# A graph layer paced by its gathers: eight stretches of nine chunks, each with one extra kind of instruction

## The chip, the cores and the metric

One core of one Trainium2 chip runs the kernel. The metric is the device time of one execution in microseconds; the time of a version is the median of its runs. All times below are of this one core.

## The reference

One graph layer with a residual and a normalisation. Each of 1,650,000 edges takes the row of its source node (160 numbers, 64 scalars and 32 vectors of 3), combines it with the edge's four attributes and small weight matrices, and adds the result to its destination node. The edges come sorted by destination: 800,000 in one direction, the same reversed, and 50,000 self-loops.

```
s, v = x[:, :64], x[:, 64:].reshape(n, 32, 3)
ss, vv = s[src], v[src]
e0, e1 = sh[:, 0:1], sh[:, 1:4]
out0 = C0 * (ss * e0 @ W1 + einsum('eui,ei->eu', vv, e1) * INV3 @ W2)
p3 = (ss @ W3)[:, :, None] * e1[:, None, :] * INV3
p4 = einsum('eui,uw->ewi', vv * e0[:, :, None], W4) * INV3
p5 = einsum('eui,uw->ewi', cross(vv, e1[:, None, :]), W5) * INV6
m = concatenate([out0, C1 * (p3 + p4 + p5)])
m_agg = segment_sum(m, dst, n)
h = m_agg through Ws and Wv
x = layernorm(x + x + relu(h))
...
```

## The kernel before

**Units, groups, pairs, chunks.** 128 edges are a unit, 6 units a group (`G`), 2 groups a pair (`PG`), 20 groups a chunk (`SG`), so a chunk has 10 pairs and 120 units. There are 1044 pairs in 105 chunks. The main loop runs over the pairs.

**One pair.** POOL issues 12 indirect DMAs (`gather`, line 398), one a unit: each brings the 128 source rows of a unit, 640 bytes each, into the tile `xg`. The pool of `xg` has four buffers, so POOL can be ahead of PE by that many pairs; each gather adds 16 to a semaphore of its own, `filled[t][j]`, with t the buffer and j the unit. PE multiplies the 12 units one after the other (`group_sums`, line 447) by the matrices `ha`, 128 edges x 128 (4 attributes x 32 slots for the destinations of a group), and sums six of them into one half of `ps`. Each of these matmuls waits for the semaphore of its unit. A matmul in fp32 appears in the profile as two weight loads and two matmuls.

**DVE.** It makes `hot` and `ha` for the next pair (`spread`, lines 419 and 422) while PE works on this one, and turns the sums of the pair before (`turn_sums`, the transpose in line 462) and adds them to `ring`, the running sums of the nodes (line 471). Once a node block of 128 is complete, PE multiplies it by the weights (`phb`, line 776), and DVE and ACT normalise it (`norm1` to `norm3`, lines 184 to 200; the square root `rstd` in line 194 is ACT's) for a store of two blocks at once (`out<-o`, line 875).

**Beside this** goes a second stream of work. Since half of the edges are the other half reversed, the kernel sorts a pack of edges into rows by DVE work (`pack`, copies and predicated copies in lines 590 to 635, with a few casts on ACT) and stores them to memory in many small DMAs on SP (`store`, line 683: `edges<-prow` of 27.8 KB and `selves<-mine` of 0.8 KB). Before a few of these stores SP loads their places into registers (line 666). This phase of stores comes back about every 1600 us.

**Order.** SP, PE, DVE and ACT run in the order in which the code is written (a manual schedule). The body of the loop issues the gathers of a pair, then goes through `group_sums`, a generator that yields after each of the 12 matmuls. After the second, DVE's `turn_sums` of the pair before is written; after the fourth, `spread` for the next pair; after each, some steps of the queued work on node blocks, loads and packs. SP issues all loads and stores of the loop. Its DMAs share eight completion lanes in turn with the few that ACT issues: a DMA waits for the one eight earlier in the program. The loads of a chunk are written 13 pairs before its first pair.

Of the kernel before, what the change touches and what calls it, by code (L numbers as in the profile page):

```python
# [39 lines left out]
F32 = mybir.dt.float32  # L40
# [6 lines left out]
ET = mybir.EngineType  # L47
# [3 lines left out]
P = 128  # L51
MUL0, MUL1 = 64, 32
D = MUL0 + 3 * MUL1
# [10 lines left out]
W = 32  # L64
# [14 lines left out]
REST = 15  # L79
ASK, OWN, QS, RUN = 8, 16, 8, 2  # L80
LEAD = 3

def plan(n_nodes, n_edges):

    nblk = 125
    assert n_nodes % nblk == 0
    assert W == FB
    nb = n_nodes // nblk
    again = 9

    per_unit = P * n_nodes / n_edges
    group = max(g for g in range(1, 17)
                if g == 1 or (g + 0.2) * per_unit + 1 + 5 * math.sqrt(g * per_unit * per_unit / P) <= W)
    head = math.ceil(min(HEAD, n_edges / (group * P)) / SG) * SG
    eh = head * group * P
    row = group * P * 3 // 2 + math.floor(per_unit * group * 3 / 2 * (1 - n_nodes / n_edges))
    assert row * n_nodes / n_edges + 5 * math.sqrt(row * n_nodes / n_edges / 16) < KM

    far = math.ceil(6 * math.sqrt(n_edges) / 2 * n_nodes / n_edges) + 2
    rows = math.ceil((n_edges - eh) / row) + 2  # L100
    ngroups = math.ceil((n_edges - n_nodes + eh * n_nodes / n_edges + far) / (group * P))
    assert eh + (rows - 1) * row - n_nodes + eh * n_nodes / n_edges - far >= ngroups * group * P
    units = P * math.ceil(max(math.ceil(n_edges / P) + again - 1, math.ceil((eh + rows * row + 1) / P)) / P)
    return nblk, nb, again, group, units, ngroups, row, head, rows, far
# [3 lines left out]
def tile_gnn_resnorm(ctx: ExitStack, tc: tile.TileContext, x, src, dst, attr, W1, W2, W3, W4, W5, Ws, Wv, out, n_edges):  # L108
    nc = tc.nc
    N = x.shape[0]  # L110
    NBLK, NB, GA, G, NU, NG, L, NH, NR, FAR = plan(N, n_edges)
# [8 lines left out]
    eps_t = const.tile([P, 1], F32, name="eps_t")  # L120
# [86 lines left out]
    def near(g):  # L207
        p = g * G * P
        return p / degree if p <= EH else EH / degree + (p - EH) / (degree - 1)
# [6 lines left out]
    for g0, g1 in parts:  # L216
        t = min((near(g) / N for g in range(g0, g1 + 1)), key=lambda t: abs(t - 0.5))
# [10 lines left out]
    TW = max(h - k * S for h, k in zip(high, seg_of)) + W  # L228
# [3 lines left out]
    with tc.tile_pool(name="once", bufs=1) as once, tc.tile_pool(name="raw", bufs=2) as rawp, \  # L232
# [5 lines left out]
            tc.tile_pool(name="psP", bufs=1, space=PSUM) as psP, tc.tile_pool(name="psA", bufs=2, space=PSUM) as psA, \  # L238
            tc.tile_pool(name="psM", bufs=2, space=PSUM) as psM, ExitStack() as later_pools:

        spotp, ownp = (later_pools.enter_context(tc.tile_pool(name=name, bufs=bufs))
                       for name, bufs in (("spot", 3), ("own", 1)))
        extremes = once.tile([P, 2, NSC], F32, name="extremes")
        count_ = once.tile([1, SG], F32, name="count")
        nc.gpsimd.iota(count_, pattern=[[1, SG]], base=0, channel_multiplier=0, allow_small_or_imprecise_dtypes=True)
# [7 lines left out]
        dq = nc.sync  # L253
# [56 lines left out]
        spot_of, spots_of, ring = {}, {}, {}  # L310
# [76 lines left out]
        filled = [[tc.alloc_semaphore(f"filled{t}_{j}") for j in range(PG * G)] for t in range(4)]  # L387
        gathers = [[0] * (PG * G) for t in range(4)]
        begun_tiles = [0]

        def gather(s, placed, u, n):

            xg = rowp.tile([P, PG * G, D], F32, name="xg")
            rows = []
            t = begun_tiles[0] % 4
            begun_tiles[0] += 1
            for j in range(n):
                part = nc.gpsimd.indirect_dma_start(  # L398
                    out=xg[:, j, :], out_offset=None, in_=x,
                    in_offset=bass.IndirectOffsetOnAxis(ap=placed[0][:, u + j:u + j + 1], axis=0))  # L400
                gathers[t][j] += 1
                key = f"gather{begun_tiles[0]}_{j}"
                part.then_inc(filled[t][j], 16)
                tc.no_tile_sem_insts.add(part.ins.name)
                tc.add_to_no_dep_group(key, part.ins)
                rows.append((xg[:, j, :], filled[t][j], 16 * gathers[t][j], key))
            return rows

        idle, sent = [], []
# [20 lines left out]
        written = {"misc": [], "ps": []}  # L430

        def fresh(kind):
            written[kind].append([])

        def wrote(kind, ins):
            ws = written[kind]
            for old in ws[-3] if len(ws) > 2 else []:
                tc.declare_no_dep(ins.ins, old, reason="its reader has waited for it")
            ws[-1].append(ins.ins)
            return ins  # L440

        def group_sums(p, rows, ha):

            ps = psA.tile([P, PG, D], F32, name="ps")
            fresh("ps")
            for j, (xr, sem, count, key) in enumerate(rows):
                mm = nc.tensor.matmul(ps[:, j // G, :], ha[:, j].rearrange("p k w -> p (k w)"), xr,  # L447
                                      start=j % G == 0, stop=j % G == G - 1)
                mm.wait_op(sem, count, "sem-ge")
                tc.declare_no_dep(mm.ins, group=key, reason="its own semaphore is waited for")  # L450
                tc.declare_fence(mm.ins, group=key)
                if j % G == 0:
                    wrote("ps", mm)
                else:
                    written["ps"][-1].append(mm.ins)
                yield ps

        def turn_sums(p, ps):
# [15 lines left out]
        C = 2 + NK  # L474
# [4 lines left out]
        def row_start(r):  # L479

            lo, hi = (math.floor(r * L * (1 - 1 / degree)) - 2 * FAR - 2, math.ceil(r * L * (1 - 1 / degree)) + 2 * FAR + 2)
            return (max(lo, 0), hi if r else 0), (max(math.floor((EH + r * L) / degree) - FAR - 2, 0),
                                                  math.ceil((EH + r * L) / degree) + FAR + 2)
# [234 lines left out]
        def own_blocks(k):  # L718

            if min((k + 1) * S, N) <= row_start(0)[1][0]:  # L720
                return []
            return list(range(k * SB, min((k + 1) * SB, nblocks)))
# [48 lines left out]
        def block(bs, h, ph):  # L771
# [3 lines left out]
            for i in range(ND):  # L775
# [4 lines left out]
        pairs = [(s, g, min(PG, NG - g, (s + 1) * SG - g)) for s in range(NSC)  # L780
                 for g in range(s * SG, min(NG, (s + 1) * SG), PG)]

        ones = once.tile([P, P], F32, name="ones")
        nc.vector.memset(ones, 1.0)

# [132 lines left out]
        def reach(s):  # L918

            end = min(NG, (s + 1) * SG) * G * P  # L920
            if s * SG < NH:
                return 0
            if s + 1 < NSC:
                end = max(end, (s * SG * G + P) * P)
            if s * SG == NH:
                end = max(end, (s * SG + W) * G * P)
            return end - EH

        packs, due = [], []
        for i in range(npacks):  # L930
# [3 lines left out]
            own = next((k for k in range(NSEG) if min((k + 1) * S, N) > row_start(i * RP)[1][0] and own_blocks(k)), NSEG - 1)  # L934
            due.append(min((first - 1) * per - 1 - LEAD, first_of[own] // PG - ASK - 1))
            packs.append(pack(i, lambda i=i: reads[i + 1]() if i + 1 < npacks else None))
# [5 lines left out]
        for k in range(1, NSEG):  # L942
            p = first_of[k] // PG
# [5 lines left out]
        for b, g in enumerate(last_of):  # L949
            p = g // PG  # L950
# [6 lines left out]
        for p, (s, g, ng) in enumerate(pairs):  # L957
            if (p + LEAD) % per == 0 and (p + LEAD) // per + 1 < NSC or not p:
                ahead_ = (p + LEAD) // per + 1
                end = reach(ahead_)  # L960
                assert end <= 0 or rows_stored[0] == NR or end <= row_start(rows_stored[0])[0][0]
                raws[ahead_] = load(ahead_)
            if p % per == 0 and s + 1 < NSC:
                after_pair(p + 1, do_cast, s + 1)
                after_pair(p + 2, do_place, s + 1)
                if s + 2 == NSC:
                    after_pair(p + 4, examine_all)
                    after_pair(p + 6, read_flags)
            rows = gather(s, placed[s], (g - s * SG) * G, ng * G)
            for j, ps in enumerate(group_sums(p, rows, has.pop(p))):  # L970
                if j == 1 and turning:
                    turn_sums(*turning)
                    turning = None
                if j == 3 and p + 1 < len(pairs):
                    s1, g1, ng1 = pairs[p + 1]
                    has[p + 1] = spread(placed[s1], (g1 - s1 * SG) * G, ng1 * G)
                work(1.0)
                if packs and p >= START:
                    when = p + (j + 1) / (ng * G)
                    todo = math.ceil(len(packs[0]) * min(1, (when - began) / max(1, due[0] - began)))  # L980
                    for step in packs[0][done:todo]:
                        if step:
                            step()
                    done = max(done, todo)
                    if done == len(packs[0]):
                        packs.pop(0), due.pop(0)
                        done, began = 0, when
# [35 lines left out]
    with tc.tile_pool(name="up", bufs=1) as up, tc.tile_pool(name="us", bufs=2) as us, tc.For_i(0, once_more, 1):  # L1023
# [3 lines left out]
        mm = up.tile([P, 2, JU], F32, name="mm")  # L1027
# [45 lines left out]
    with tc.tile_pool(name="edges2", bufs=2) as ep, tc.tile_pool(name="ops2", bufs=2) as op, \  # L1073
            tc.tile_pool(name="node2", bufs=1) as np_, tc.tile_pool(name="psA2", bufs=2, space=PSUM) as psA, \
            tc.tile_pool(name="psF2", bufs=1, space=PSUM) as psF:
        with tc.For_i(0, blocks, 1) as b:
# [5 lines left out]
            with tc.For_i(u0, u1, GA) as u:  # L1082
# [21 lines left out]
                ps = psA.tile([NBLK, 2, 512], F32, name="ps2")  # L1104
                for j in range(GA):
                    for h in range(2):
                        nc.tensor.matmul(ps[:, h, 0:2 * D], hot[:, j, :], xa[:, j, 2 * h:2 * h + 2, :],
                                         start=j == 0, stop=j == GA - 1)
# [11 lines left out]
            i = 0  # L1120
# [44 lines left out]
```

## Time and profile before

| what | value |
|---|---|
| median of 3 runs | 17920.9 us (17918.87 to 17925.29) |
| the profiled execution | 18022.02 us, span 18020.3 us |
| PE | 6860.2 us, 38% of the span |
| PE's weight loads | 6095.4 us, 34% |
| DVE | 7478.3 us, 41% |
| ACT | 171.6 us, 1% |
| POOL | 11866.1 us, 66% |
| clock of PE granted | 0.627 |
| DMA | 74 GB/s over the span |

The page gives the busy time of each engine; PE's weight loads run beside its matmuls. A group of instructions is listed by line, engine, operation and tiles, with its count, its busy time, the mean of one in ns, and the idle time of the engine just before it with what ended it. "issue" there means that nothing which the profile shows was waited for. `q0` is the queue of the gathers, `q1` that of SP's and ACT's transfers.

By the places of the chunks' first gathers, the stretches that the change touches lie, in us from the start of the span, at 1443 to 2989 (A), 3504 to 5050 (B), 5564 to 7111 (C), 7623 to 9172 (D), 9687 to 11233 (E), 11751 to 13293 (F), 13812 to 15358 (G) and 15874 to 17414 (H).

### The profile page before, as it was taken

What the parts mean: (1) busy time and instruction counts of PE and PEld (TensorE: products, weight loads), DVE (VectorE), ACT (ScalarE), POOL (GpSimd) and SP (SyncE); (2) the same over time, 40 slices, a digit from 0 to 9 for tenths busy, and PEclk for the clock granted to TensorE, in tenths of its full rate; (3) what the DMA queues carried; (4) which work ended last, traced back from release to release, by engine and by line L of the source; (5) the groups of instructions that cost most, each with busy time, mean ns of one, the idle gap of its engine ahead of it and who ended that gap; (6) DMA issues with size and microseconds to landing.
All of it is one profiled execution on the core that took longest, in us unless ns stands there. A gap on an engine that the chain in (4) does not pass through costs nothing. (4 is left out here: it accounts for less than half of the span.)

```text
span 18020.3 us, 93561 instructions
## 1 busy us (share of the span) xinstructions
PE 6860.2 (38%) x28971; PEld 6095.4 (34%) x28972; DVE 7478.3 (41%) x12038; ACT 171.6 (1%) x273; POOL 11866.1 (66%) x12535
## 2 busy tenths in 40 slices
PE   3333334333333333333333333333333333333433
PEld 2233333333333333333333333333333333333333
DVE  7344245334524442453344345434433452444232
ACT  0000000000000000000000000000000000000000
POOL 6566666666666666666666666666666666666666
PEclk6666666666666666666666666666666666666666
DMA  2222322322332233223223322332232233222222
GB/s 72 79 71 78 79 68 73 83 76 70 77 81 70 71 80 77 70 73 85 73 70 78 80 70 72 82 77 69 72 85 74 69 76 78 72 70 71 75 72 61
DMA packets 740962, 1341.57 MB, mean 74 GB/s; under 512 B 243310, under 2 KB 522674, under 8 KB 725894
## 3 DMA queue, kind: packets, MB, share of 16 engines
q0 software_dynamic: 601056, 1026.60, 23.5%
q1 hardware_dynamic: 138138, 308.06, 5.6%
q8 instruction: 231, 3.78, 0.1%
q14 instruction: 273, 2.24, 0.0%
q10 hardware_dynamic: 1264, 0.88, 0.0%
HBM read 1263.28 MB, written 71.42 MB: 74 GB/s over the span
## 5 line engine op out<-in xcount | busy, mean ns | idle before, releaser
L398 POOL DMA_INDIRECT xg<-in_x,si x12522 | 11862.6, 947 | 6108.8 <-issue 3663.5
L447 PE MATMUL ps<-xg,ha 128*128 128x160 f32 x25044 | 6282.8, 397 | 9643.7 <-issue 5600.4
L447 PEld LDWEIGHTS ps<-xg,ha 128*128 128x128 f32 x25044 | 5409.4, 267 | 10356.9 <-issue 10352.3
L462 DVE STREAM_TRANSPOSE sums<-ps 128x320 f32<-128x320 f32 x1044 | 527.0, 505 | 6249.8 <-remote 4712.4
L422 DVE TENSOR_TENSOR ha<-hot,pk 128x1536 f32<-128x1536 f32 x1044 | 1830.4, 1753 | 52.1 <-remote 11.0
L776 PE MATMUL phb<-BWk,ring 128*128 128x160 f32 (+1 forms) x3910 | 1176.4, 381 | 1441.0 <-issue 858.6
L184 DVE SCALAR_TENSOR_TENSOR y<-phb,xt 128x320 f32<-128x320 f32 x196 | 95.9, 489 | 3623.2 <-PE ps L447 2504.7
L776 PEld LDWEIGHTS phb<-BWk,ring 128*128 128x128 f32 (+1 forms) x3910 | 894.1, 258 | 1489.1 <-issue 886.9
L471 DVE TENSOR_TENSOR ring<-ring,sums 128x160 f32 x2087 | 684.5, 328 | 253.1 <-issue 158.6
L419 DVE TENSOR_TENSOR hot<-bank,rel 128x384 f32<-128x384 f32 x1044 | 570.6, 547 | 67.4 <-DMA xt<-in_x 67.3
L632 DVE COPY_PREDICATED prow<-marks,prow 128x2370 f32<-128x2370 int32 (+5 forms) x198 | 550.3, 2780 | 1.1
L766 DVE STREAM_TRANSPOSE ring<-xr 128x1280 f32<-128x1280 f32 x188 | 437.2, 2326 | 0.1
L632 DVE COPY_PREDICATED pra<-marks,pra 128x1580 f32<-128x1580 int32 (+5 forms) x198 | 378.8, 1913 | 0.0
L763 DVE TENSOR_TENSOR xr<-xr,bank 128x1280 f32<-128x1280 f32 x188 | 276.5, 1471 | 4.6 <-DVE bank L756 1.4
L194 ACT ACTIVATE rstd<-mv,eps_t 128x2 f32<-128x2 f32 x196 | 58.0, 296 | 16997.5 <-DVE mv L189 12612.7
L468 DVE TENSOR_TENSOR ring<-ring 128x196 f32<-128x196 f32 (+20 forms) x485 | 149.4, 374 | 1.8
L200 DVE TENSOR_SCALAR o<-y,mv,rstd 128x160 f32<-128x160 f32 x391 | 130.2, 374 | 10.9 <-remote 1.6
L629 DVE COPY_PREDICATED_SCALAR hit<-marks,none 128x395 int32 (+5 forms) x198 | 130.1, 657 | 10.9 <-DVE pri L627 3.2
L716 DVE MEMSET ring<- 128x1280 f32 (+1 forms) x98 | 119.3, 1218 | 23.1 <-issue 21.0
L188 DVE BATCH_NORM_STATS2 st<-y 128x6 f32<-128x160 f32 x391 | 121.7, 311 | 6.7
L630 DVE COPY_PREDICATED hit<-marks,pri 128x395 int32<-128x395 int32 (+5 forms) x198 | 118.5, 598 | 10.4 <-issue 2.2
L627 DVE TENSOR_TENSOR pri<-hit,marks 128x395 int32<-128x395 int32 (+11 forms) x198 | 113.5, 573 | 14.8 <-issue 3.2
(346 smaller groups left out, 1752.7 us busy)
## 6 DMA issues: line engine op xcount, KB each, us to landing
xg<-in_x,si POOLq DMA_INDIRECT x12522
xr<-in_x SPq DMA_DIRECT2D x93, 1280.0 KB
r<-edges SPq DMA_DIRECT2D x100, 384.0 KB
edges<-prow SPq DMA_DIRECT2D x1330, 27.8 KB
xt<-in_x SPq DMA_DIRECT2D x195, 160.0 KB
out<-o SPq DMA_DIRECT2D x195, 160.0 KB
pra<-in_attr SPq DMA_DIRECT2D x10, 2370.0 KB
selves<-mine SPq DMA_DIRECT2D x1328, 0.8 KB
```

The source lines that it names most:

```text
L200: nc.vector.tensor_scalar(o[:n, i], y[:n, i], mv[:n, i, 0:1], rstd[:n, i:i + 1], op0=ALU.subtract, op1=ALU.mult)
L398: part = nc.gpsimd.indirect_dma_start(out=xg[:, j, :], out_offset=None, in_=x, in_offset=bass.IndirectOffsetOnAxis(ap=placed[0][:, u + j:u ...
L419: idle[:] = [nc.vector.tensor_tensor(hot[:, :n], slotsP[:, 0:W].unsqueeze(1).to_broadcast([P, n, W]), rel[:, u:u + n].unsqueeze(2).to_broa ...
L422: nc.vector.tensor_tensor(ha[:, :n], hot[:, :n].unsqueeze(2).to_broadcast([P, n, NK, W]), pk[:, :, u:u + n].rearrange("p k u -> p u k").un ...
L447: mm = nc.tensor.matmul(ps[:, j // G, :], ha[:, j].rearrange("p k w -> p (k w)"), xr, start=j % G == 0, stop=j % G == G - 1)
L462: nc.vector.transpose(at[:, :ng], ps[:, :ng].rearrange("p g (b f) -> p g b f", f=FB))
L468: nc.vector.tensor_tensor(ring[k][:, b, :past], ring[k][:, b, :past], ring[k - 1][:, b, S:S + past], op=ALU.add)
L471: nc.vector.tensor_tensor(here, here, at[:, i], op=ALU.add)
L632: nc.vector.copy_predicated(what[:n, a:e], mi[:, r].unsqueeze(2).to_broadcast([n, e - a, what.shape[2]]), what[:n, a + d:e + d])
L763: nc.vector.tensor_tensor(xr[:, r], xr[:, r], sumP[:, r].unsqueeze(2).to_broadcast([P, r.stop - q, D]), op=ALU.mult)
L766: nc.vector.transpose(here[:, r], xr[:, r].rearrange("p q (b f) -> p q b f", f=FB))
L776: wrote("misc", nc.tensor.matmul(ph[:nb], ring[k][:, i, cols], BWk[:, i, :], start=i == 0, stop=i == ND - 1))
```

## The change

From chunk 8 on, of every 12 chunks the first nine get one addition and the next three none. The additions are in order:

- A: the 12 gathers of a pair add to one semaphore, and only the pair's first matmul waits, for all 12.
- B: eight more matmuls a pair with a matrix of zeros, `nought`, into the same sums: 720 in all.
- C: three DMAs a pair on SP that load 16 rows of 128 bytes into an unused tile, `junk`: 270.
- D: twelve DMAs a pair on SP that load one such row: 1080.
- E: 24 memsets of one column a pair on DVE: 2160.
- F: 24 copies of one column a pair on ACT: 2160.
- G: register loads on SP, whose values nothing uses. The built program has 191 register loads on SP before and after, of which 187 are those of the stores.
- H: three DMAs a pair as in C, on ACT's queue: 270.

```diff
+ADDED = "ABCDEFGH"
+
+def added(s):
+    i, j = divmod(s - 8, 12)
+    return ADDED[i] if 0 <= i < len(ADDED) and j < 9 else None
...
                 gathers[t][j] += 1
+                one = added(s) == "A"
+                if one:
+                    gathers[t][j] -= 1
+                    gathers[t][0] += 1
                 key = f"gather{begun_tiles[0]}_{j}"
-                part.then_inc(filled[t][j], 16)
+                part.then_inc(filled[t][0 if one else j], 16)
...
+            if one:
+                rows = [(r[0], filled[t][0] if not j else None, 16 * gathers[t][0], r[3]) for j, r in enumerate(rows)]
             return rows
...
-                mm.wait_op(sem, count, "sem-ge")
+                if sem:
+                    mm.wait_op(sem, count, "sem-ge")
...
+                kind = added(pairs[p][0])
+                if kind == "B" and 0 < j % G < G - 1:
+                    written["ps"][-1].append(nc.tensor.matmul(ps[:, j // G, :], nought, xr, start=False, stop=False).ins)
+                if kind == "C" and j % 4 == 3:
+                    junk = junkp.tile([16, 32], F32, name="junk")
+                    dq.dma_start(junk, x[0:16, 0:32])
+                if kind == "D":
+                    junk = junkp.tile([16, 32], F32, name="junk")
+                    dq.dma_start(junk[0:1], x[0:1, 0:32])
+                if kind == "E":
+                    nc.vector.memset(bits[:, 0:1], 0.0)
+                    nc.vector.memset(bits[:, 1:2], 0.0)
+                if kind == "F":
+                    nc.scalar.copy(bits[:, 2:3], eps_t)
+                    nc.scalar.copy(bits[:, 3:4], eps_t)
+                if kind == "G":
+                    nc.values_load_multi_w_load_instructions(
+                        spots_of[pairs[p][0]][0:1, 0:4], engines=[ET.SP], min_val=0, max_val=TW - W,
+                        skip_runtime_bounds_check_because="held within bounds")
+                if kind == "H" and j % 4 == 3:
+                    junk = junkp.tile([16, 32], F32, name="junk")
+                    nc.scalar.dma_start(junk, x[0:16, 0:32])
                 yield ps
```

The tiles `nought` (128 x 128, zeroed once), `bits` (128 x 4) and 16 buffers of `junk` are new. With the added lines, line 398 becomes 404, 447 becomes 459, 462 becomes 497, 471 becomes 506, 683 becomes 718, 776 becomes 811.

PE where stretch B begins (`ps` are the sums of a pair, `phb` the products of a node block). Before:

```order
L447 MATMUL ps<-xg,ha 128x160
L776 MATMUL phb<-BWk,ring 128x160
L447 MATMUL ps<-xg,ha 128x160 x51
L776 MATMUL phb<-BWk,ring 128x160
L447 MATMUL ps<-xg,ha 128x160
```

After, from the same row of 51 on:

```order
L811 MATMUL phb<-BWk,ring 128x160
L459 MATMUL ps<-xg,ha 128x160 x28
L471 MATMUL ps<-xg,nought 128x160
L459 MATMUL ps<-xg,ha 128x160
L471 MATMUL ps<-xg,nought 128x160
L459 MATMUL ps<-xg,ha 128x160
L471 MATMUL ps<-xg,nought 128x160
L459 MATMUL ps<-xg,ha 128x160
L471 MATMUL ps<-xg,nought 128x160
L459 MATMUL ps<-xg,ha 128x160 x3
```

Behind each but the first and last of a group's six matmuls now stands a matmul with zeros.

DVE in the middle of a pair of stretch E (`sums` are the turned sums of the pair before, `ha` the matrices of the next). Before:

```order
L462 STREAM_TRANSPOSE sums<-ps 128x320
L471 ISA
L471 TENSOR_TENSOR ring<-ring,sums 128x5x32
L471 ISA
L471 TENSOR_TENSOR ring<-ring,sums 128x5x32
L419 TENSOR_TENSOR hot<-bank,rel 128x384
L422 TENSOR_TENSOR ha<-hot,pk 128x1536
L590 SCALAR_TENSOR_TENSOR hit<-prow,marks 128x395
```

After:

```order
L497 STREAM_TRANSPOSE sums<-ps 128x320
L506 ISA
L506 TENSOR_TENSOR ring<-ring,sums 128x5x32
L506 ISA
L506 TENSOR_TENSOR ring<-ring,sums 128x5x32
L479 MEMSET bits 128x1
L480 MEMSET bits 128x1
L479 MEMSET bits 128x1
L480 MEMSET bits 128x1
L431 TENSOR_TENSOR hot<-bank,rel 128x384
L434 TENSOR_TENSOR ha<-hot,pk 128x1536
L479 MEMSET bits 128x1
```

Four memsets now stand between the adds and `hot`, four more stand ahead of the transpose, and 16 behind `ha`.

More of the change, by code (lines that the diff above doesn't have):

```diff
@@ L239, in tile_gnn_resnorm @@
             tc.tile_pool(name="psM", bufs=2, space=PSUM) as psM, ExitStack() as later_pools:
-        spotp, ownp = (later_pools.enter_context(tc.tile_pool(name=name, bufs=bufs))
-                       for name, bufs in (("spot", 3), ("own", 1)))
+        spotp, ownp, junkp = (later_pools.enter_context(tc.tile_pool(name=name, bufs=bufs))
+                              for name, bufs in (("spot", 3), ("own", 1), ("junk", 16)))
         extremes = once.tile([P, 2, NSC], F32, name="extremes")
@@ L781, in tile_gnn_resnorm @@
                  for g in range(s * SG, min(NG, (s + 1) * SG), PG)]
+        nought = once.tile([P, P], F32, name="nought")
+        nc.vector.memset(nought, 0.0)
+        bits = once.tile([P, 4], F32, name="bits")
         ones = once.tile([P, P], F32, name="ones")
```

## The prediction

> **What bounds the kernel now.** I read the groups of the page first, for what one pair of groups costs each engine, then the waits of POOL and PE, for who holds up whom, and then a table of the eight stretches that the change touches.
>
> ```profile
> L398 POOL DMA_INDIRECT xg<-in_x,si x12522 | 11862.6, 947 | 6108.8 <-issue 3663.5
> L447 PE MATMUL ps<-xg,ha 128*128 128x160 f32 x25044 | 6282.8, 397 | 9643.7 <-issue 5600.4
> L447 PEld LDWEIGHTS ps<-xg,ha 128*128 128x128 f32 x25044 | 5409.4, 267 | 10356.9 <-issue 10352.3
> L462 DVE STREAM_TRANSPOSE sums<-ps 128x320 f32<-128x320 f32 x1044 | 527.0, 505 | 6249.8 <-remote 4712.4
> ```
>
> POOL's line is the bound: (11862.6 + 6108.8) / 12522 = 1.435 us for each gather, 17.2 us for the twelve of a pair, and 12522 of them fill the span of 18020.3 us. PE stands idle 9643.7 us ahead of its matmuls and DVE 6249.8 us ahead of its transposes, so neither is short of time. The idle time of POOL divides as follows (waiter, releaser: us in total, times, longest):
>
> ```profile
> POOL xg L398 <- issue: 3663.5, 12020, 1.7
> POOL xg L398 <- PE ps L447: 1220.3, 220, 33.2
> POOL xg L398 <- remote: 1201.7, 275, 6.9
> ```
>
> The first row is the ordinary gap of 0.30 us between two gathers; the other two are about 495 stalls at the first gather of a pair, where the buffer of four pairs earlier has to be free. Without them a gather would take 0.947 + 0.305 = 1.25 us. That looks like a kernel held by PE. Whether it is decides this forecast, so here is the same quantity where the engines do unlike amounts of other work. The columns are the stretch, its length, the busy time and count of PE, of its weight loads, of DVE, ACT and POOL, and then clock and DMA; the rows are the stretches A to H.
>
> ```profile
> 1443.00:2989.00 1546.00, 603.07 (x2500) 538.88 (x2500) 634.22 (x1027) 14.94 (x23) 1021.84 (x1080) 0.63 0.30 76
> 3504.00:5050.00 1546.00, 588.42 (x2490) 526.75 (x2491) 650.60 (x1040) 14.94 (x23) 1022.61 (x1080) 0.62 0.30 76
> 5564.00:7111.00 1547.00, 593.19 (x2508) 523.13 (x2507) 653.76 (x1036) 6.01 (x19) 1022.52 (x1081) 0.63 0.29 75
> 7623.00:9172.00 1549.00, 586.18 (x2498) 523.71 (x2499) 653.25 (x1039) 14.98 (x23) 1023.07 (x1081) 0.62 0.29 76
> 9687.00:11233.00 1546.00, 588.87 (x2500) 521.91 (x2500) 641.61 (x1033) 14.94 (x23) 1023.00 (x1080) 0.62 0.30 76
> 11751.00:13293.00 1542.00, 603.14 (x2499) 533.02 (x2499) 656.43 (x1049) 14.91 (x23) 1022.58 (x1081) 0.63 0.30 75
> 13812.00:15358.00 1546.00, 590.95 (x2504) 527.07 (x2502) 651.08 (x1035) 6.02 (x19) 1021.69 (x1080) 0.63 0.29 74
> 15874.00:17414.00 1540.00, 602.04 (x2535) 529.09 (x2536) 593.58 (x962) 5.03 (x17) 1023.79 (x1081) 0.62 0.29 72
> ```
>
> 1080 gathers take 1540 to 1549 us in every stretch, 1.43 us each, with 962 to 1049 DVE instructions. SP's work varies far more. Two windows of 680 us, the first in the middle of a store phase (D holds it), the second outside one, give POOL's line and the DMAs of each, in that order:
>
> ```profile
> L398 POOL DMA_INDIRECT xg<-in_x,si x475 | 449.8, 947 | 230.4 <-issue 138.6 <-remote 54.0 <-PE ps L447 37.8
> edges<-prow SPq DMA_DIRECT2D x128, 27.8 KB
> selves<-mine SPq DMA_DIRECT2D x128, 0.8 KB
> q0 software_dynamic: 22719, 38.83, 23.7%
> q1 hardware_dynamic: 5964, 16.15, 6.8%
> ```
>
> ```profile
> L398 POOL DMA_INDIRECT xg<-in_x,si x476 | 451.2, 948 | 229.9 <-issue 139.8 <-PE ps L447 47.4 <-remote 42.6
> q1 hardware_dynamic: 4248, 8.85, 4.8%
> ```
>
> 256 more small transfers in 680 us, 1716 more packets, and one gather fewer. So the pace of 1.43 us belongs to the gathers, not to what engines or queues do beside them; the stalls fill up whatever POOL's 1.25 us leaves of it. I forecast from that. Its weak side, a pattern in which PE's signals arrive late, is the first rival.
>
> **The change part by part.** Each stretch is 90 pairs; one pair lasts 17.2 us.
>
> A: one wait a pair instead of twelve, 990 fewer waiting matmuls on PE. PE's own waits say what they cost:
>
> ```profile
> PE ps L447 <- DVE ha L422: 3280.4, 462, 61.0
> ...
> PE ps L447 <- DMA xg<-in_x,si: 1.0, 2, 0.6
> ```
>
> 1.0 us in the whole run is lost on gathers: PE comes to a pair after its rows have landed. Now the first matmul needs the twelfth row, at most 11 × 1.43 = 15.7 us later than it does now, once, since three other buffers keep POOL going. I take 0; the ends are -209 us (third rival) and +15.7 us.
>
> B: eight zero matmuls a pair, two passes each by the count x25044 for 12522 units, so 16 passes. At the 267 ns of a weight load that is 4.3 us a pair on a PE with 588 us busy in the 90 pairs, 6.5 us a pair: 10.8 of 17.2 us. They wait for nothing new. Hidden by PE's idle time; ends 0 and 4.3 × 90 = 384 us, and I take 0, because PE need only keep the pace of the gathers.
>
> C, D and H: 270 loads of 16 rows on SP, 1080 of one row on SP, 270 of 16 rows on ACT's queue. SP has room: 12 DMAs at the 0.228 us of the row below are 2.7 us of a pair. The price of the low end is that of the store phase, one gather of 1.43 us for 256 transfers, 5.6 ns each: 1.5 + 6.0 + 1.5 = 9 us. The high end charges a packet like a gather's (second rival). I take the low end; its row is of the same kind as D's loads, one row and under 1 KB. Each of these DMAs also waits for the one eight earlier in the shared completion lanes. Behind a late one stand, on SP, a chunk's loads, written 13 pairs or 224 us ahead of their use, and on ACT the next rstd. No row of before shows ACT's queue in the middle of the run. The Trainium skill, DMA: Bandwidth & Descriptors, "Issuing engines are not separate DMA queues", says that DMAs started from ScalarE, SyncE or GpSimd end on the same 16 engines and interleave, so by it H costs what C costs; no run here has shown that yet, and without it H stays between 0 and the second rival's share of it.
>
> E and F: 24 memsets on DVE and 24 copies on ACT a pair, of one column. The nearest rows are these, with the small DMA of SP:
>
> ```profile
> L560 DVE MEMSET cum<- 128x1 f32 x11 | 0.6, 59 | 0.0
> L303 ACT CAST ff<-fi 128x1 f32<-128x1 int32 x4 | 0.7, 184 | 3.6 <-issue 3.5
> L683 SPq DMA_DIRECT2D selves<-mine x1411: 2/228/1409, 471.6 to 16850.6; - x177
> ```
>
> E is 24 × 59 ns = 1.4 us of DVE on top of 642 / 90 = 7.1 us a pair; F is 24 × 184 ns = 4.4 us of an ACT that is busy for 14.91 us of that stretch's 1542. Queued behind the memsets are the transpose and the products ha that PE waits for. Behind the copies is only the rstd of a node block, and the copies wait for nothing but each other, so ACT has them done before DVE reaches that block. Covered by DVE's 6249.8 us of idle and ACT's; without that cover E would be 127 us and F 397 us. I take 0 for both. One page bears on E: the Trainium skill, SBUF — State Buffer, "Who interferes with whom", has DVE instructions with two SBUF inputs shut out a GpSimd instruction that reads SBUF, but none with at most one input; a memset has none, so by it the gathers would not feel E, and with the opposite rule E would be 127 us.
>
> G: the built order holds 187 register loads on SP for the stores before and after, and none beside them that is new, so G is the unchanged program: 0.
>
> Sum: 9 us on the profiled execution's 18022 us. That execution is 0.56% above the median of 17920.9 us, so the forecast is 17920.9 + 9 = 17930 us.
>
> **The rivals.** First, slower: PE's bursts. Around one stall the rows of SP, POOL, DVE and PE (start, length, then in brackets the idle time before) are
>
> ```profile
> 8321.08 0.69 SPq L683 DMA_DIRECT2D selves<-mine  x1
> 8331.61 0.23 SPq L683 DMA_DIRECT2D selves<-mine  x1
> 8331.86 0.94 POOL L398 DMA_INDIRECT xg<-in_x,si  x1 [4.48 <-remote]
> 8331.62 0.52 DVE L462 STREAM_TRANSPOSE sums<-ps 128x320 f32<-128x320 f32 x1 [23.19 <-remote]
> 8304.27 9.05 PE L447 MATMUL ps<-xg,ha 128*128 128x160 f32 x47 [3.21 <-DVE ha L422]
> 8335.27 6.06 PE L447 MATMUL ps<-xg,ha 128*128 128x160 f32 x26 [20.89 <-DVE ha L422]
> ```
>
> PE ended its burst by 8314, yet DVE's transpose starts at 8331.62, when POOL has paused; meanwhile an SP instruction takes 0.69 us instead of 0.23. Handovers get through when POOL pauses, so PE works two pairs in one burst, 47 passes in 9.05 us, 0.193 us each. B adds 16 × 0.193 = 3.1 us a pair to it. If the pause must grow by that, 278 us: 18210 us; if by half, 18070 us, which I take as its value. It decides once work left over after a burst exceeds what PE gets done between bursts. E would pay its 127 us in the same way. Against it: PE has 20.89 us idle between two bursts, and if late records made the pattern, the unprofiled runs would not have it. Chance 0.24.
>
> Second, slower: the packets share one capacity with the gathers. 22719 / 475, about 48 packets a gather in 1.43 us, are 30 ns a packet; with 16 packets for each load of C and H and one for D, 9720 packets × 30 ns = 290 us, 18211 us. The store phase speaks against it: 1716 packets for 1.43 us, 0.8 ns each. Chance 0.13, with a partial price likelier than the whole, 18050 us.
>
> Third, faster: A's waits are what makes PE late. Then the stalls vanish there: (1220.3 + 1201.7) / 12522 = 0.193 us a gather, 1080 of them 209 us, 17712 us. The 1.0 us of waits on gathers speaks against it, and so does the constant pace. Chance 0.06.
>
> **How the numbers follow.** Everything hidden: 0.55, 17895 to 17957 us. The rest, 0.02, is a mishap of the lanes, slower. From no change a measurement here tells about 0.2%, 36 us. So faster 0.07 (with a sliver of the first case), same 0.54, slower 0.39. The range runs from 17895 to 18160 us: it holds the first case and most of the two slower ones, and leaves out the third rival and their far ends, under 2 in 10.
>
> **What would show it.** Eight stretches of 1080 gathers at 1540 to 1550 us each would show every step right. B or E longer by 100 us or more, with longer stalls on PE, is the first rival; C and H longer by over 40 us with an unchanged D is the second; A at 1.25 us a gather is the third. TENSOR_LOADs on SP in G beyond the store's would make my reading of the order wrong. The forecast is wrong if the pace of 1.43 us is set by the engines' exchange and not by the gathers.

## The result: 112 us slower, and the profile after

The changed kernel takes 18032.81 us (median of 3, 18025.04 to 18040.93) against 17920.9 us: 1.0062 times as long, 95% interval 1.0039 to 1.0085. The forecast was 17930 us in a range of 17895 to 18160 us, with "same" as the likeliest outcome; the time lies in the range, on the slower side, 103 us above the forecast.

One thing has to be cleared up before the traces are compared. The two profiles shown, of 18022.02 us before and 18032.81 us after, differ by 11 us, the medians by 112. The kernel before took 17920.9 us where it was first timed and 18017.7, 18016.0 and 17998.2 us (medians) on the three chips of the experiments. The changed kernel, 18032.81 us in its first runs, took 18133.35 us when it was run again. So a program differs by some 100 us between chips or sessions, more than the two profiles differ, and the first ones' chip is not on record. The profile of before belongs with the slower times, that of the changed kernel with the faster. So the profile of before is set beside a profile of the changed kernel from a chip on which the kernel before took 18017.7 us. Its table of the stretches A to H, in the columns of the prediction's, is this:

```profile
1451.00:2993.00 1542.00, 590.35 (x2485) 523.48 (x2484) 632.21 (x1027) 14.93 (x23) 1023.36 (x1079) 0.63 0.30 76
3510.00:5069.00 1559.00, 805.23 (x3860) 712.55 (x3861) 651.70 (x1039) 14.98 (x23) 1021.02 (x1076) 0.68 0.30 75
5590.00:7142.00 1552.00, 593.06 (x2502) 526.34 (x2501) 653.12 (x1034) 6.03 (x19) 1025.16 (x1081) 0.62 0.30 75
7655.00:9256.00 1601.00, 559.45 (x2493) 511.75 (x2492) 653.08 (x1039) 15.04 (x23) 1025.53 (x1081) 0.63 0.29 73
9775.00:11328.00 1553.00, 557.36 (x2488) 519.09 (x2486) 701.65 (x3109) 14.97 (x23) 1025.82 (x1080) 0.64 0.30 76
11842.00:13398.00 1556.00, 580.10 (x2496) 522.17 (x2497) 652.03 (x1039) 317.89 (x2161) 1025.04 (x1080) 0.62 0.30 75
13917.00:15471.00 1554.00, 582.22 (x2503) 520.39 (x2502) 652.70 (x1035) 6.02 (x19) 1024.87 (x1080) 0.63 0.29 73
15982.00:17545.00 1563.00, 592.26 (x2539) 519.40 (x2539) 593.73 (x962) 5.04 (x17) 1028.01 (x1083) 0.62 0.29 72
```

Measured between the starts of gathers, from the last gather before a stretch to the stretch's last, the stretches change by -2 (A), +13 (B), +6 (C), +53 (D), +8 (E), +10 (F), +9 (G) and +18 us (H), 114 us together. A wait at an end of a stretch can fall on either side of the cut: measured from a stretch's first gather to the first one behind it, B and F come out at +19 and +15. D and H are each one event and a small rest; the others are a few us each, and G, which I had called the unchanged program, is among them. POOL's line in that profile has 36 us more of busy time and 92 us more of idle time than the line of before (11862.6 and 6108.8 us):

```profile
L404 POOL DMA_INDIRECT xg<-in_x,si x12522 | 11898.4, 950 | 6201.0 <-issue 3754.6
```

In the profile of the changed kernel's first runs, the groups and POOL's waits that answer to those shown of before are

```profile
L404 POOL DMA_INDIRECT xg<-in_x,si x12522 | 11892.7, 950 | 6098.8 <-issue 3735.5
L459 PE MATMUL ps<-xg,ha 128*128 128x160 f32 x25044 | 6216.9, 391 | 9156.7 <-issue 5454.6
L497 DVE STREAM_TRANSPOSE sums<-ps 128x320 f32<-128x320 f32 x1044 | 527.8, 506 | 5957.1 <-remote 4632.6
L471 PE MATMUL ps<-xg,nought 128*128 128x160 f32 x1440 | 401.0, 355 | 196.0 <-issue 195.2
L482 ACT COPY bits<-eps_t 128x1 f32<-128x1 f32 x1080 | 206.6, 191 | 317.3 <-ACT bits L483 251.9
```

```profile
POOL xg L404 <- issue: 3735.5, 12013, 16.1
POOL xg L404 <- remote: 1272.3, 310, 6.7
POOL xg L404 <- PE ps L459: 1048.1, 186, 32.7
```

PE and DVE are still idle 9157 and 5957 us ahead of their main groups. (POOL's sums in it are not to be set against those of before for the 112 us, since these two executions differ by 11 us.) No engine has become the bound, and yet the time has grown.

### The profile page after: what moved, and what is told of

It reads as the page before. It is cut to its first block, busy times and chain, and to the rows that moved or that the text cites. A ratio compares the mean times of both kernels' runs of the same rounds, so it can differ in the third digit from the quotient of the medians.

```text
span 18031.1 us, 103492 instructions
## 1 busy us (share of the span) xinstructions
PE 6979.3 (39%) x30411; PEld 6241.5 (35%) x30412; DVE 7556.8 (42%) x14199; ACT 473.7 (3%) x2433; POOL 11896.2 (66%) x12535
## 5 line engine op out<-in xcount | busy, mean ns | idle before, releaser
L459 PE MATMUL ps<-xg,ha 128*128 128x160 f32 x25044 | 6216.9, 391 | 9156.7 <-issue 5454.6
L459 PEld LDWEIGHTS ps<-xg,ha 128*128 128x128 f32 x25044 | 5336.0, 263 | 9795.2 <-issue 9781.1
L471 PE MATMUL ps<-xg,nought 128*128 128x160 f32 x1440 | 401.0, 355 | 196.0 <-issue 195.2
L471 PEld LDWEIGHTS ps<-xg,nought 128*128 128x128 f32 x1440 | 298.7, 233 | 221.7 <-issue 221.2
L482 ACT COPY bits<-eps_t 128x1 f32<-128x1 f32 x1080 | 206.6, 191 | 317.3 <-ACT bits L483 251.9
L483 ACT COPY bits<-eps_t 128x1 f32<-128x1 f32 x1080 | 206.0, 191 | 328.6 <-ACT bits L482 275.3
L479 DVE MEMSET bits<- 128x1 f32 x1080 | 63.7, 59 | 233.9 <-DVE bits L480 120.6
```

What stands on the lines that cost most here:

```text
L471: written["ps"][-1].append(nc.tensor.matmul(ps[:, j // G, :], nought, xr, start=False, stop=False).ins)
L482: nc.scalar.copy(bits[:, 2:3], eps_t)
```

## The experiments

Two theories went in. Theory 1: the time is in single late transfers, in D and H, and the rest is the difference between chips. Theory 2, later called N: every instruction that any engine executes costs the gathers' pace a few ns, even where its engine has time to spare.

**1. The changed kernel again.** No edit.

> The changed kernel again, beside the kernel before on the same chip. Theory 1 (one late transfer): the two profiles differ by 32 us in D, where POOL stands once for 32.7 us because SP, behind with its own DMAs, issues the load xr late and DVE waits for it, by about 13 us once in H, and by nothing clear elsewhere; then the times should differ by 11 to 50 us, 0.06 to 0.3%, and the 112 us between the two medians came with the chip or the session. Theory 2 (a price in every stretch that the profile of before hides): the difference is 112 us, 0.6%, again.

18133.35 against 18017.74 us: +115.6 us, ratio 1.0066 (1.0052 to 1.008). The 112 us are the change's; theory 1 alone falls.

**2. D alone.**

```diff
-    return ADDED[i] if 0 <= i < len(ADDED) and j < 9 else None
+    return "D" if i == 3 and j < 9 else None
```

> Only stretch D has its addition (1080 loads of one row on SP, nine chunks); the other seven additions are out. Theory 1: about 30 us slower than before, 0.2%, with the one stall of POOL near 8600 us in the profile. Theory 2: only D's share, no more than a seventh to a third of the 112 us, and a stretch D that is longer by the same amount in every chunk and not in one.

18064.67 us, +46.9 us, ratio 1.0028 (1.0017 to 1.0038). That is more than theory 1's 30 us and more than theory 2's third of 112, but it lies in one place, as theory 1 has it: the chunks outside D keep their times (they change by 0.0 us in the mean), and D has one stall. SP's loads of `sa` and `xr` for that place (line 746 in before, 781 here), first of before and then of this run, and then the waits of DVE, PE and POOL in this run:

```profile
8479.23 0.86 SPq L746 DMA_DIRECT2D sa<-selves  x1
8480.10 0.71 SPq L746 DMA_DIRECT2D xr<-in_x  x1
```

```profile
8627.34 0.59 SPq L781 DMA_DIRECT2D sa<-selves  x1
8628.50 0.55 SPq L781 DMA_DIRECT2D xr<-in_x  x1
...
8630.30 0.22 DVE L790 TENSOR_TENSOR sa<-sa,bank 128x64 f32<-128x64 f32 x1 [42.42 <-DMA sa<-selves]
8652.01 1.49 DVE L798 TENSOR_TENSOR xr<-xr,bank 128x1280 f32<-128x1280 f32 x1 [21.22 <-DMA xr<-in_x]
...
8660.59 5.38 PE L459 MATMUL ps<-xg,ha 128*128 128x160 f32 x24 [69.06 <-DVE ha L434]
...
8666.24 0.95 POOL L404 DMA_INDIRECT xg<-in_x,si  x1 [45.86 <-PE ps L459]
```

Read from the top: SP, in a store phase and with twelve more DMAs a pair, issues `xr` 148 us later than before; DVE waits 42 and 21 us; `ha` is late, PE stands 69 us; POOL, four buffers ahead at most, stands 46 us. That one stall is D's price. POOL's line over the whole run is worth a look too:

```profile
L404 POOL DMA_INDIRECT xg<-in_x,si x12522 | 11899.5, 950 | 6119.4 <-issue 3666.3
```

The gathers were busy 37 us longer than in before, all through the run, and yet the chunks outside D are no longer: shorter waits of POOL made up for it.

**3. All but D.** The expression of experiment 1 with `and i != 3`.

> All additions but D's. Theory 1: within 20 us of before, with no stall over 20 us between 8500 and 8700 us. Theory 2: 70 to 100 us slower than before.

18126.34 us (five runs from 18088.55 to 18132.21), ratio 1.0058 (1.0044 to 1.0071), +108.6 us. Theory 1 falls a second time, and theory 2's 70 to 100 us are passed. The two parts, 47 and 109 us, come to more than the 116 us of the whole. In the profiled run, 38 us faster than this median, the stretches grow by 14 (B), 5 (C), 10 (E), 8 (F), 9 (G) and 15 us (H), D by nothing.

**4. B in 96 chunks.**

```diff
+    return "B" if 8 <= s < 104 else None
```

> Only the zero matmuls of B, but in all chunks from 8 to 103, 960 pairs instead of 90, so that B's price is seen ten times over. Theory 1 and the forecast: the same time as before within 40 us, since PE needs only keep the pace of the gathers. Rival of the forecast (PE's bursts grow by 16 passes of 0.193 us a pair, half of it paid): 1.5 us a pair, 1500 us slower. Theory 2 with B as its carrier: 4.6 to 112 us in nine chunks are 50 to 1200 us here.

18151.62 us, +133.9 us, ratio 1.0073 (1.0058 to 1.0089). Spread evenly: 1.4 us a chunk, no chunk over 8 us. That is 0.14 us a pair for 16 more passes, not the 1.5 of the rival and not the 0 of the forecast. The sizes of programs now matter; the page's first lines of before and of this run read

```profile
span 18020.3 us, 93561 instructions
```

```profile
span 18152.5 us, 124282 instructions
```

30721 instructions more: 4.4 ns for each. POOL's line says where the time lies:

```profile
L404 POOL DMA_INDIRECT xg<-in_x,si x12522 | 11896.0, 950 | 6216.1 <-issue 3634.8
```

POOL is idle 107 us longer than in before, in the waits at the first gather of a pair: all but the "issue" part comes to 2581 against 2445 us. Its busy time is 33 us longer, as it was by 37 in experiment 2 with only 1081 instructions more, so this part does not follow the count.

**5 and 6. Many small memsets or few large.** E in 96 chunks; then the two memsets of one column replaced by

```diff
+                    if j % 3 == 0:
+                        nc.vector.memset(bits[:, 0:256], 0.0)
```

> Only E's addition, in all chunks from 8 to 103: 24 memsets of one column a pair, 23040 in all. The forecast (the pace belongs to the gathers, DVE's idle time covers them): within 36 us of before. Theory N (every executed instruction takes some 4 ns of the gathers' pace, whatever its engine; by E's stretch in the last profiles 8.5 us for 2160): 80 to 100 us slower, spread evenly over the chunks.

> In all chunks from 8 to 103, four memsets of 256 columns a pair on DVE, at every third unit, in place of 24 of one column: about the same DVE time in a sixth of the instructions, 3840 in all. Theory N (a price per instruction): 16 us slower than before. Theory B (a price for DVE's busy time, or for its writes): as much as the kernel with 24 small memsets, 80 to 100 us.

The small ones: 18102.88 against 18016.01 us, +86.9 us, ratio 1.0051 (1.0036 to 1.0066). The large ones: 18024.68 us, +8.7 us, 1.0004 (0.9995 to 1.0014), which can be told neither from nothing nor from the 16 us of theory N. The rows (count: shortest/median/longest ns) of one of the two small memsets, and of the large one:

```profile
L479 DVE MEMSET bits<- x11520: 59/59/59, 1498.3 to 18068.4; 128x1 f32 x199
```

```profile
L480 DVE MEMSET bits<- x3840: 272/272/272, 1496.9 to 17964.5; 128x256 f32 x192
```

2 x 11520 x 59 ns are 1.36 ms of DVE, 3840 x 272 ns are 1.04 ms: three quarters of the work in a sixth of the instructions, at a tenth of the price. On DVE it is the count that is paid for, not the time. 23032 more instructions on the page make 3.8 ns each.

**7. Instructions that do nothing.** G in 96 chunks.

> Only G's addition in all chunks from 8 to 103. The register loads themselves are not in the program, but one semaphore instruction for each is, 12 a pair on SP, 11520 in all: they do no work, and nearly all of them only raise a semaphore. Theory N at 4 ns: 46 us slower. By G's own stretch in the last profiles (8.7 us for 1080, 8 ns each): 93 us. Theory B (busy time): no difference, since SP does nothing else by them. The forecast: no difference.

18129.83 us, +113.8 us, ratio 1.0066 (1.0051 to 1.0082), the runs from 18102.7 to 18145.31 us: more than the 46 us of theory N and the 93 by G's own stretch. This is what G is:

```profile
L485 SPq EVENT_SEMAPHORE  x11520: 1/17/1676, 1437.6 to 18036.0; - x199
```

No register is loaded, but a semaphore instruction was left for each load, 17 ns long. In the profiled run, the fastest of the four, two chunks grow by 24 and 11 us, with `xr` late at the first (DVE waits 25.45 us for it); the other 94 grow by 0.5 us each, 50 us for 11520, 4.3 ns. So the price per instruction holds on SP too, for instructions with no work, as far as this one profile shows it, and on top of it SP falls behind in a store phase. The median of the runs is 27 us longer than this profile's run; how much of that is such events was not seen.

**8. D outside the store phases.**

```diff
+    return "D" if s in (42, 43, 44, 45, 51, 52, 53, 54, 55) else None
```

> Only D's addition, still nine chunks and 1080 loads of one row, but in chunks 42 to 46 and 51 to 55, of which none but a sliver has a store phase. Theory 1 for D (SP falls behind in the store phase, and the one late load xr stops DVE, PE and POOL): the stall of 46 us disappears, and what is left is the price of the instructions, 5 to 12 us. If D's price belongs to its DMAs as such: 47 us as in the run with D alone.

18025.80 us, +9.8 us, 1.0006 (0.9997 to 1.0015), and no stall over 8 us at those places. The same 1080 DMAs cost 47 us in a store phase and 10 us or nothing outside. (The edit leaves out chunk 46, which the expectation names.)

**9. A in 96 chunks.** 10560 waits fewer, no instruction fewer.

> Only A's change, in all chunks from 8 to 103: one waiting matmul a pair in place of twelve, 10560 waits fewer and no instruction fewer. Theory N (a price for each executed instruction): no difference, within 10 us. If a wait on a semaphore has a price of its own: by A's stretch in the last profiles, 2.3 us less for nine chunks, 25 us faster. Third rival of the forecast (the stalls vanish): 2200 us faster.

17989.53 against 17998.2 us: -8.7 us, 0.9995 (0.9986 to 1.0004). No difference that can be told; the waits alone are not worth 25 us.

**10. Zero matmuls over few columns.** B in 96 chunks, `ps[:, j // G, 0:8]` and `xr[:, 0:8]`.

> B's zero matmuls in all chunks from 8 to 103, over 8 of the 160 columns: as many instructions on PE as in the run with B in all chunks, 7680 matmuls, each two weight loads and two passes, and less PE time. Theory N: again about 134 us slower. Theory B (PE's busy time, its longer bursts): clearly less, 134 x (16 thin passes against 16 full ones), some 80 us or under.

18142.37 us, +144.2 us, 1.0081 (1.0065 to 1.0096), 4.7 ns for each of the same 30721 instructions. It agrees with theory N, but it does not exclude PE's time as the cause. First the run with full columns, then this one:

```profile
L471 PEld LDWEIGHTS ps<-xg,nought x15360: 186/190/338, 1491.5 to 18119.8; 128*128 128x128 f32 x200
L471 PE MATMUL ps<-xg,nought x15360: 296/299/633, 1492.2 to 18120.0; 128*128 128x160 f32 x200
```

```profile
L471 PEld LDWEIGHTS ps<-xg,nought x15360: 186/337/338, 1496.7 to 18093.1; 128*128 128x128 f32 x200
L471 PE MATMUL ps<-xg,nought x15360: 169/221/381, 1497.4 to 18093.1; 128*128 128x8 f32 x200
```

The passes became shorter (221 for 299 ns), the weight loads longer (337 for 190 ns, at a granted clock of 0.589 for 0.678), so PE's time did not fall as I had meant it to.

**11. Fewer instructions than before.** The matmuls of the pairs read only the upper half of each number.

```diff
-ha[:, j].rearrange("p k w -> p (k w)"), xr,
+ha[:, j].rearrange("p k w -> p (k w)").bitcast(BF16)[:, 1::2], xr.bitcast(BF16)[:, 1::2],
```

> No addition. The matmuls of the pairs take only the upper half of each fp32 number (as bf16), so that each is one weight load and one pass instead of two of each: some 25000 instructions of PE fewer in the profile, and half its time there; gathers, waits and all other work stay, and the sums have the precision of the halves. The forecast (gathers alone set the pace): the same time as before. Theory N at 4.4 ns: 110 us faster. Theory of PE's bursts: faster by more, 24 passes a pair fewer out of 47 in a burst of 9 us, up to the whole of the stalls, 2400 us.

17846.61 against 17998.2 us: -151.6 us, ratio 0.9916 (0.9901 to 0.9931). Its page begins with

```profile
span 17842.3 us, 68517 instructions
```

25044 instructions fewer at 6.1 ns each, the right sign and more than the 110 us expected. POOL's line is

```profile
L404 POOL DMA_INDIRECT xg<-in_x,si x12522 | 11902.4, 951 | 5910.6 <-issue 3697.5
```

POOL's idle time falls by 198 us against before, while its busy time is 40 us longer. So the gain lies in POOL's waits, not in the gathers. But most of the 2400 us of stalls stay: PE halves its work and POOL still waits. It is faster than both kernels, at the precision of bf16 in these products; whether it was the count or PE's time that paid, this run alone doesn't say, since both fell by half.

**12. H in 96 chunks.**

> Only H's addition, three loads of 16 rows a pair on ACT's queue, in all chunks from 8 to 103, 2880 in all. Theory N at the 5 us that C's and H's stretches cost outside one event: 50 us slower, spread evenly. Beside it, theory L (the lanes that SP shares with ACT delay SP's load xr in a store phase): a stall of POOL of 10 us or more in several of the nine store phases, as once near 16900 us, 50 to 100 us more. The forecast: 16 us.

18495.58 us, +497.4 us, ratio 1.0273 (1.0258 to 1.0289), ten times the even price. It isn't even: 19 chunks take some 478 us of it, and the other 77 grow by under 0.1 us each, with 2880 DMAs in all. The stalls lie in and just after the store phases. SP's waits in this run and ACT's queue in one stretch:

```profile
SPq L913 <- DMA junk<-in_x: 1565.8, 21, 102.7
...
SPq L718 <- DMA junk<-in_x: 304.3, 24, 82.7
```

```profile
11901.58 7.06 ACTq L490 DMA_DIRECT2D junk<-in_x  x15
11987.27 0.29 ACT L200 ACTIVATE rstd<-mv,eps_t 128x2 f32<-128x2 f32 x1 [85.40 <-DVE mv L195]
11987.27 6.99 ACTq L490 DMA_DIRECT2D junk<-in_x  x15
12108.65 0.30 ACT L200 ACTIVATE rstd<-mv,eps_t 128x2 f32<-128x2 f32 x1 [121.09 <-DVE mv L195]
```

ACT issues its small loads in lots of 15, each behind an `rstd` for which it has waited 85 to 121 us. SP's DMAs wait, through the shared lanes, for a load of ACT's that has not been issued: up to 102.7 us for a store. In a store phase, where SP has no time to lose, its `xr` is then late, as in D. Theory L held, with 19 chunks instead of several and 478 us instead of 50 to 100.

## Why the prediction was right in its range and wrong in its steps

- **The range** held by luck. The 9 us of the sum and the 17930 us were off by more than 100, and the upper part of the range was kept for the first two rivals, neither of which came. The time came to lie there through terms that the prediction had put at nothing.
- **The bound** held in part. PE, DVE and ACT do stay idle for long with B, E and F, the first rival's half price (139 us for B) is ten times the 13 us measured, and the third rival's 209 us for A came to -2 us. But "the pace of 1.43 us belongs to the gathers" is not what the runs show. A gather with its ordinary gap takes 1.25 us, and the rest of the 1.43 is POOL's waits. The prediction let these fill up what is left; they are the part that moves: +107 us of idle time in experiment 4, -198 in experiment 11, while 37 us of slower gathers in experiment 2 cost nothing outside D. The prediction's own last sign of being wrong, a pace set by the engines' exchange, is nearer to this, though not in the size of the first rival.
- **"I take 0" for B, E and F** is the first failure. The price is not that of the engine's time but of the instruction: 3.8 to 4.7 ns in experiments 4, 5, 7 (its even part) and 10, 6.1 ns downward in 11. In nine chunks that is 13, 8 and 10 us. The row of the store phase, "one gather of 1.43 us for 256 transfers", would even have given some 3 ns for each instruction, since at least 256 register moves stood beside them; but one gather is the smallest difference that such a count can show, so its nearness to 4 ns is luck.
- **G "is the unchanged program"** was a misreading. The list of the built program that I read has no semaphore instructions in it; 1080 of them were there, for 9 us.
- **D at 6 us** is the largest failure: 53 us in the whole kernel, 47 alone. The term "SP has room: 12 DMAs are 2.7 us of a pair" took SP's dense speed. In the store phase an instruction of SP takes 0.69 us between two bursts, a row that the prediction quotes under another rival, and five of its DMAs in a row start 2.8 us apart (8318.28 to 8329.47 us of before); SP is behind there already. Outside such a phase the 1080 loads cost 10 us, near the 6.
- **C at 1.5 us and H at 1.5 us**: C measured 5 to 6 us, H 18, of which one stall of 20.3 us, most of it new, is the lanes' doing. I had named what stands behind a late DMA in the lanes, and priced it at nothing but a 0.02 mishap. The Trainium skill, DMA: Bandwidth & Descriptors, "Issuing engines are not separate DMA queues", is borne out for the transfers themselves: in experiment 12 H's chunks without a stall grew by under 0.1 us, no more than C's. The wait between the issuing engines came on top, and it was the larger part by far.
- **The second rival** falls: at 30 ns a packet C alone would have paid 129 us.
- **The memsets and the port**: the Trainium skill, SBUF — State Buffer, "Who interferes with whom", has a DVE instruction with at most one SBUF input, outside the two-port modes, not contend with GpSimd, so a memset passes beside a gather. Experiment 6 agrees, with 3840 memsets of 272 ns at a price that cannot be told from nothing (+8.7 us).
- **"0.56% above the median"**, read as the profile's own excess, was most likely the difference between two chips or sessions: on the three chips of the experiments the kernel before took 17998.2 to 18017.7 us.

The sum as it should have been, with the stalls sized by the stretches of experiment 1: 9931 more instructions on the page (103492 against 93561) at 4.4 ns are 44 us; D's 53 us less 5 for its 1080 instructions are a stall of 48, and H's 18 less 1 for its 270 are 17. That is 109 us of the 112 to 116 measured. It is fitted to the runs, and C and G cost some 5 and 4 us more than their instructions at 4.4 ns, for which no run gives a reason.

What stays open is why an instruction of an idle engine costs POOL 4 ns. These rows of before bear on it:

```profile
15780.27 0.42 PE L447 MATMUL ps<-xg,ha 128*128 128x160 f32 x1 [2.38 <-issue]
15781.06 0.94 POOL L398 DMA_INDIRECT xg<-in_x,si  x1 [0.30 <-issue]
...
15783.07 0.42 PE L447 MATMUL ps<-xg,ha 128*128 128x160 f32 x1 [2.38 <-issue]
...
15788.31 0.94 POOL L398 DMA_INDIRECT xg<-in_x,si  x1 [6.31 <-remote]
...
15791.56 3.97 PE L447 MATMUL ps<-xg,ha 128*128 128x160 f32 x28
```

Ahead of POOL's wait PE's passes start 2.8 us apart, though PE waits for nothing that the profile shows; after POOL has stood for 6.31 us, 28 of them run in 3.97 us while POOL issues again. So much of what the page counts as PE's idle time is not time to spare: in such a stretch every instruction comes late, whatever its own length. That added instructions lengthen POOL's pauses in this way is a reading of these rows and was not tested. On DVE the price may also pass through the order: in experiment 5, 3597.6 us of PE's waits are put down to the memsets. All the runs of the experiments carry the profiler's times, so it can't be told from them whether the cost is the instruction's own or that of its record; and for PE alone, count and time were not separated.

## What to carry to other kernels

Where one engine's DMA issues seem to set the pace and all others seem free, count instructions and not only busy time: here a thousand extra ones on PE, DVE, ACT or SP cost about 4 us, and halving PE's gave 0.8% back. Ask also how much of a steady pace is waiting: a pace that holds through eight stretches does not show that the engine at its head sets it. A queue that only issues DMAs has a budget of its own that busy time does not show; look for the phase in which it runs behind, since that is where an extra DMA becomes a stall of everything. And a small load on another engine's queue is not free of the first queue if the two share completion lanes: its issue waits in its engine's order, and the first queue waits for it.

## What was not expected of the hardware

A semaphore instruction with no work, 17 ns long, costs 4.3 ns of a pace that its engine has no part in (experiment 7, the even part), about as much as a memset (3.8 ns) or one weight load or pass of PE (4.4 ns, where time and count were not separated). And the same program ran 0.4 to 0.6% apart on different chips or in different sessions (17920.9 and 17998.2 to 18017.7 us; the changed kernel 18032.81 and 18133.35 us), almost as much as the whole change.
